# Four changes of order in a one-core kernel: reciprocals behind the key matrices, the gates' series in three parts, the last layer's turns further apart, the last fetch of W_out sooner

## The chip, the cores and the metric
The kernel runs on one core of one Trainium2 chip. The metric is the device time of one execution in microseconds; before, the median of three runs is 3143.19 us (3143.12 to 3145.72). The core has a matmul engine (TensorE, PE), three engines for elementwise work (VectorE or DVE, ScalarE or ACT, GpSimd or POOL), and a fifth, SyncE (SP), which here issues nearly all DMAs. Each of them takes its instructions from a queue of its own, in order, and they wait for each other through semaphores.

## The reference, cut to what matters
Inputs are x (4 x 512 x 512), fside of the same shape, a condition vector per batch, and weights. All is 32-bit floating point. Two layers follow each other:

```python
# layer 1: a bidirectional "wkv" scan, then gated delta-rule attention
ek = exp(min(k, 30)); ekv = ek * v                    # k = v = fside
nf, df = scans of (ekv, ek) forward: a = a*decay + in # nb, db: backward
num = nf + nb - ekv + euk*v;  den = df + db - ek + euk
c = sigmoid(x) * num / max(den, 1e-8) * (0.8 + 0.2*tf)
q, k, v, z = split(c @ W_qkvz.T);  b, a = split(c @ W_ba.T)
q, k, v = silu(causal_conv4(q, k, v))
beta = sigmoid(b);  g = -exp(A_log) * softplus(a + dt_bias)
# 16 query/key heads, 32 value heads, chunks along the sequence:
M = strictly_lower((beta*k) @ k.T * decay);  T = inverse(I + M)
v_c, k_c = T @ (beta*v), T @ (beta*k*exp(g))
for each chunk:                                       # the recurrent part
    v_new = v_c - k_c @ state
    o = (q*exp(g)) @ state + (q @ k.T * decay) @ v_new
    state = state*exp(g_last) + (k*exp(g_last-g)).T @ v_new
x = x + (norm_w * rmsnorm(o) * silu(z)) @ W_out.T
# layer 2: the wkv scan again (r is the new x), then a binarized linear layer
c2 = sigmoid(x) * num2/den2 * (0.8 + 0.2*tf)
x = x + c2 @ (sign(W) * mean|W|).T + bias
```

## The kernel before, in words
The attention is cut into 64 units: one unit is one batch and one query/key head with its two value heads (number n = 16*batch + head). A unit takes the whole sequence of 512 as four chunks of 128. A Python loop runs i from 0 to 65, and each iteration is a list of 22 slots (0 to 21), `plan`, in which steps of different units are interleaved: the key side of unit i+6 (K), convolutions, inverse and queries of unit i (F), the chunk recurrence of unit i-1 (C, four chunks of steps `chunk_r`, `chunk_w`, `chunk_t`), the output norm and its transposes of unit i-2 (O), and the product with W_out of unit i-3 (W). `last_step` ends the work on the last unit and the last batch.

The order in which instructions are issued is written out by hand: the helper class `InOrder` (line 80 is its line, which is why nearly every row of the profile has L80) hands each instruction to its engine and keeps program order. The tile framework places a few instructions otherwise, among them the selects of `gap_mask` on POOL, which it puts where it takes their data to be there.

Steps that matter here:

- `gap_load(n, "d")` (SP) fetches the decay exponents of unit n into tile dkd; `gap_mask` (POOL) masks them, `gap_exp` (ACT) exponentiates. `key_pairs` (PE) makes k·kᵀ in the one PSUM bank of tag "inv", tile ps_kk. `key_root` (POOL) computes the norms' roots and br, nbr, nbe. `key_matrix` (DVE, two halves of four operations) multiplies ps_kk, nbr and dkd into M, and frees the bank. `queries` (PE) then uses that bank for q·kᵀ, tile ps_kq. `key_blocks` (SP) stores M's diagonal blocks, `inverse_load` fetches blocks of the inverse.
- Work of the wkv scan is spread over iterations: heads 3, 4, 5, 7 of a batch carry a 128-column slice of layer 1's scan for the next batch, heads 9, 11, 12, 13 one of layer 2's scan for the same batch; 28 iterations in all. `wkv_under` prepares the denominator, `wkv_over` takes its reciprocal in two halves of 128 x 256 (tile f), `wkv_end` multiplies (into cT for layer 1; for layer 2 it also stores the result, "base", to DRAM).
- The gates of the next batch (beta and g) are computed at head 8, in iterations 8, 24 and 40: `gates_product` (PE, tile ps_ba), `gates_exp`, `gates_series` (DVE: the reciprocal of 1 + exp(-b), and softplus by a series; tiles sp_e, sp_s, sp_p, sp_y), `gates_sum` (PE, ps_g from sp_y), `gates_keep`, `gates_turn` (ps_gt), `gates_rows`. Batch 0's gates are made before the loop.
- `chunk_r` (PE, ps_s) multiplies the state; `chunk_r_end` (DVE) makes r, which `chunk_w` (PE, ps_w) needs.
- Layer 2 is done by `job`s, steps hung onto iterations and slots: `fw_load`, `fw_abs`, `fw_sign` (DVE, fa), `fw_turn` (PE, ps_fw) and `fw_end` prepare the binarized weight in iterations 58 and 59; batches 0 to 2 are finished in iterations 60, 62 and 64 and the one after each: `last_turn` (PE transposes, ps_lx, four per batch), `last_sigmoid` (ACT, sg), `last_mix` (POOL, last_c), `last_product` (PE, ps_f), `last_add` (DVE, then a store on SP). `last_base` and `last_load` fetch their inputs. The last batch is finished in `last_step`.
- `out_start(n, h)` (SP) fetches half h of unit n's rows of W_out (tile wo, two buffers); it stands in slots 13 and 15 for unit O, `out_product` (PE, ps_out) uses it.

PSUM has two banks of tag "pp", three of "pj" (which ps_lx, ps_h, ps_fw, ps_out, ps_g, ps_gt share), one of "inv" and two of "st".

Of the kernel before, what the change touches and what calls it, by code (L numbers as in the profile page):

```python
# [12 lines left out]
ALU = mybir.AluOpType  # L13
# [12 lines left out]
def bc(ap, axis, n):  # L26

    ap = ap.unsqueeze(axis)
    shape = list(ap.shape)
    shape[axis] = n  # L30
    return ap.to_broadcast(shape)
# [9 lines left out]
def kernel(  # L41
# [26 lines left out]
    NC = S // P  # L68
# [14 lines left out]
    V, A, G, T, Q = (InOrder(e) for e in (nc.vector, nc.scalar, nc.gpsimd, nc.tensor, nc.sync))  # L83
    NB = P // BS
    NM = 2 * NC
    NU = B * HQ
# [33 lines left out]
    for i in range(3):  # L120
        t = const.tile([P, NM, P], F32, name=f"inv_t{i}")
        G.memset(t, 0.0)
        inv_t.append(t)
        t = const.tile([P, NM // 2, 3 * BS], F32, name=f"inv_n{i}")
# [21 lines left out]
    with ExitStack() as main:  # L146
# [13 lines left out]
        xs, cT, beta, gsum, eg = {}, {}, {}, {}, {}  # L160
# [40 lines left out]
        nea = const.tile([P, HV], F32, name="nea")  # L201
# [113 lines left out]
        def gates_tile(g, name, tag):  # L315
            t = wkp.tile([P, S], F32, tag=tag, name=f"sp_{name}_{g['b']}")
            return t[:, : NC * HV].rearrange("p (c h) -> p c h", c=NC)
# [13 lines left out]
            V.scalar_tensor_tensor(e, y, -1.0, y, ALU.mult, ALU.min)  # L331
            A.activation(e, e, AF.Exp)

        def gates_series(g):

            b, y, e = g["b"], g["y"], g["e"]
            V.tensor_scalar_add(beta[b], beta[b], 1.0)
            V.reciprocal(beta[b], beta[b])
            s = gates_tile(g, "s", "d")
            V.tensor_scalar_add(s, e, 2.0)  # L340
            V.reciprocal(s, s)
            V.tensor_tensor(s, s, e, ALU.mult)
            V.tensor_tensor(e, s, s, ALU.mult)
            p = gates_tile(g, "p", "ekv")
            V.tensor_scalar_mul(p, e, 1.0 / 19.0)
            for odd in (17, 15, 13, 11, 9, 7, 5, 3):
                V.scalar_tensor_tensor(p, p, 1.0 / odd, e, ALU.add, ALU.mult)
            V.scalar_tensor_tensor(p, p, 1.0, s, ALU.add, ALU.mult)
            V.tensor_scalar_max(y, y, 0.0)
            V.scalar_tensor_tensor(y, p, 2.0, y, ALU.mult, ALU.add)  # L350
            V.tensor_tensor(y, y, bc(nea, 1, NC), ALU.mult)

        def gates_sum(g):
            n = NC * HV
# [680 lines left out]
        def last_add(b, c):  # L1035
# [7 lines left out]
        K, F, C, O, W = AHEAD, 0, -1, -2, -3  # L1043
# [10 lines left out]

            [(slab_turn, K, 1), (out_product, W, 2), (out_product, W, 3), ("wkv", wkv_copy),
             (inverse_1_end, F), (out_scale, O, 0), (gap_exp, F, "t", 0), (chunk_squares, C, 0),
             ("gate", gates_series), ("sub", 2, 22)],

            [(chunk_r, C, 1), (inverse_2, F), (out_add, W, 2),
             (chunk_r_end, C, 1), (out_add, W, 3), (slab_end, K, 1), (chunk_q_end, C, 1),  # L1060
             (gap_exp, F, "t", 1), ("sub", 3, 23)],

            [(project, K, 1, 0), (slab_turn, F, 2), ("wkv", turn_slice, "x"),
             (inverse_2_end, F), (out_scale, O, 1), ("wkv", wkv_bound), ("sub", 4, 24)],

            [(chunk_w, C, 1), (project, K, 1, 1), (head_turn, O, 0), ("gate", gates_sum), (chunk_w_end, C, 1),
             (slab_end, F, 2), ("wkv", wkv_exp), ("wkv", wkv_x),
             (slab_start, F, 3), ("sub", 5, 25)],

            [(project, F, 2, 0), (tap, K, 1, 0), (taps, K, 1), (head_end, O, 0),  # L1070
             ("gate", gates_keep), ("wkv", wkv_mix), ("sub", 6, 26)],

            [(chunk_t, C, 1), (inverse_3, F), ("gate", gates_turn), (chunk_t_end, C, 1), (silu, K, 1),
             ("wkv", wkv_scan, "d", False), (slab_start, F, 0), ("sub", 7, 27)],

            [(project, F, 2, 1), (head_turn, O, 1), (slab_turn, F, 3), ("gate", gates_rows), (inverse_3_end, F), ("wkv", wkv_scan, "d", True),
             (square, K, 1), (chunk_squares, C, 1), ("sub", 8, 28)],

            [(chunk_r, C, 2), (inverse_4, F), (norms, K, 1), (tap, F, 2, 0), (head_end, O, 1), (slab_end, F, 3), (tap, F, 2, 1),
             (chunk_r_end, C, 2), (tap, F, 2, 2), (tap, F, 2, 3), (norms_copy, K, 1), (chunk_q_end, C, 2),  # L1080
             ("wkv", wkv_sum, "d"), (slab_start, C, 4), (slab_start, C, 5), ("sub", 9, 29)],

            [(project, F, 3, 0), (norms_turn, K, 1), (slab_turn, F, 0), (inverse_4_end, F), (silu, F, 2),
             ("wkv", wkv_scan, "n", False), ("sub", 10, 30)],
# [11 lines left out]

            [(chunk_r, C, 3), (key_pairs, K), (tap, F, 0, 0), (slab_end, C, 5), (turn_end, F, 1),
             (tap, F, 0, 1), (chunk_r_end, C, 3), (tap, F, 0, 2), (tap, F, 0, 3),
             (chunk_q_end, C, 3), (inverse_load, F + 1), ("wkv", wkv_over, 0), ("sub", 15, None)],

            [(z_product, C, 0, 0), (turn, F, 3), (key_matrix, K, 0), (silu, F, 0),
             ("wkv", wkv_over, 1), ("sub", 16, None)],

            [(chunk_w, C, 3), (z_product, C, 0, 1), (out_turn, O, 0), (chunk_w_end, C, 3),
             (turn_end, F, 3), (square, F, 0), (key_matrix, K, 1), ("wkv", wkv_end),
             (gap_load, K + 1, "d"), (slab_start, K + 1, 1), ("sub", 17, None)],

            [(z_product, C, 1, 0), (out_turn, O, 1), (out_end, O, 0), (key_blocks, K), ("sub", 18, None)],

            [(chunk_t, C, 3), (norms, F, 0), (queries, F), (z_silu, C, 0), (out_end, O, 1),  # L1110
             ("sub", 19, None)],

            [(z_product, C, 1, 1), (chunk_t_end, C, 3), (norms_copy, F, 0), (queries_end, F, 0), (queries_end, F, 1),
             (chunk_squares, C, 3), (gap_load, F + 1, "t"), ("sub", 20, None)],
# [17 lines left out]
        for pool, tag, count, shape in (  # L1132
# [3 lines left out]
            for i in range(count):  # L1136
                t = pool.tile(shape, F32, tag=tag, name=f"lent_{tag}_{i}")
# [6 lines left out]
        for pool, tag, shape in ((u1p, "nz", [P, NC, 2, HD]), (u1p, "hT", [P, 2, S])):  # L1144
            t = pool.tile(shape, F32, tag=tag, name=f"lent_{tag}")
# [101 lines left out]
        g = {"b": 0}  # L1247
# [44 lines left out]
        first_key(0)  # L1292
        gates_exp(g)
        first_key(1)
        gates_series(g)
        gates_sum(g)
        first_conv(0)
        gates_keep(g)
# [61 lines left out]
        def job(i, slot, f, *args):  # L1360
            jobs.setdefault((i, slot), []).append((f, args))
# [3 lines left out]
        for n in range(KT):  # L1365
            i, slot = at + n // 2, 9 * (n % 2)
            job(i - (slot == 0), (slot - 4) % 22, fw_load, n)
            for more, f in ((0, fw_abs), (1, fw_sign), (3, fw_turn), (4, fw_end)):
                job(i, slot + more, f, n)
        for b in range(B - 1):  # L1370
            i = at + 2 + 2 * b
            for half in range(2):
                job(i - 1, 15 + half, last_base, b, half, b == 0)
            for c in range(NC):
                job(i - 1, 15, last_load, b, c)
                for more, f in ((5, last_turn), (6, last_sigmoid), (8, last_mix)):
                    job(i, more + c, f, b, c)
                late, slot = ((0, 13), (0, 17), (1, 2), (1, 4))[c]
                job(i + late, slot, last_product, b, c)
                job(i + late, slot + 1, last_add, b, c)  # L1380
        for half in range(2):
            job(NU + 1, 6, last_base, B - 1, half, False)

        def last_step():
            n = NU - 1
# [10 lines left out]
        for i in range(NU - W - 1):  # L1396
            b, hq = divmod(i, HQ)
            w, soon = extra(i), extra(i + 1)
            g = {"b": b + 1} if hq == GATES and b + 1 < B else None

            s, half = (i + 2) // GROUP, (i + 2) % GROUP
            s = s if s and half < 2 and s * GROUP < NU else None
            later = []
            for slot, line in enumerate(plan):
                for f, *rest in line:
                    if f == "wkv":
                        if w:
                            rest[0](w, *rest[1:])
                    elif f == "soon":
                        if soon:  # L1410
                            rest[0](soon, *rest[1:])
                    elif f == "gate":
                        if g:
                            rest[0](g)
                    elif f == "load":
                        if s is not None and half == 0:
                            group_load(s)
                    elif f == "sub":
                        if s is not None and rest[half] is not None:
                            group_step(s, rest[half])  # L1420
                    elif f == "store":
                        if s is not None and half == 1:
                            group_end(s)
                    elif 0 <= i + rest[0] < NU:
                        if i == 0 and (f in INVERSE or f == gap_load and rest[0] > K):
                            later.append((f, *rest))
                        elif i or f != inverse_load:
                            f(i + rest[0], *rest[1:])
                for f, args in jobs.get((i, slot), ()):
                    f(*args)  # L1430
                if i == 0 and slot == 13:
                    for n in others:
                        first_matrix(n)
                if i == 0 and slot == 18:
                    for f, *rest in later:
                        f(rest[0], *rest[1:])
# [33 lines left out]
```

## Time and profile before
| | |
|---|---|
| median of 3 runs | 3143.19 us |
| the profiled execution | 3145.25 us, its span 3143.2 us |
| mean granted PE clock | 0.982 of full |
| PE busy | 2991.7 us, 95% |
| DVE / ACT / POOL busy | 66% / 59% / 42% |
| startup (span start to iteration 1) | 196.3 us, of it 75.2 us PE idle |
| an iteration of batch 1 or 2 without extra work | 43.16 us |
| with a slice of layer 1's / layer 2's scan | 45.66 / 45.17 us |
| iterations 8, 24, 40 (gates) | 53.52, 50.79, 50.79 us |
| iterations 58, 59, 60, 62 | 43.24, 47.21, 52.11, 48.05 us |
| iteration 64 and the tail | 87.39 us |

A row of a timeline reads: start and duration in us, engine, line, operation, out<-in by tile names, shapes, how many instructions the row stands for, and in brackets the idle time just before it with what ended it. A row of the waits reads: the waiting engine and tile, what it waited for, then total time, times and the longest in us. DVE's busy time does not say what bounds: an engine that is off PE's path may be idle or late without cost, until PE waits for it.

### The profile page before, as it was taken

What the parts mean: (1) busy time and instruction counts of PE and PEld (TensorE: products, weight loads), DVE (VectorE), ACT (ScalarE), POOL (GpSimd) and SP (SyncE); (2) the same over time, 40 slices, a digit from 0 to 9 for tenths busy, and PEclk for the clock granted to TensorE, in tenths of its full rate; (3) what the DMA queues carried; (4) which work ended last, traced back from release to release, by engine and by line L of the source; (5) the groups of instructions that cost most, each with busy time, mean ns of one, the idle gap of its engine ahead of it and who ended that gap; (6) DMA issues with size and microseconds to landing.
All of it is one profiled execution on the core that took longest, in us unless ns stands there. A gap on an engine that the chain in (4) does not pass through costs nothing.

```text
span 3143.2 us, 57926 instructions
## 1 busy us (share of the span) xinstructions
PE 2991.7 (95%) x20058; PEld 1979.9 (63%) x20058; DVE 2066.1 (66%) x4738; ACT 1861.3 (59%) x5115; POOL 1313.4 (42%) x3044
## 2 busy tenths in 40 slices
PE   6489999999999999999999999999999999999998
PEld 3256666666666666666666666666666666665664
DVE  7546767667665777668766776667765656577642
ACT  2446666666666666556665666566666666655542
POOL 3216354263522646164432646255442515255302
PEclk9689999999999999999999999999999999999999
DMA  3334544444434323332332422332332322333321
GB/s 75 90 87 140 144 122 127 119 141 132 137 111 142 111 68 92 95 94 85 108 104 89 126 69 88 109 91 84 114 94 74 113 83 84 110 89 96 105 84 54
DMA packets 421875, 320.52 MB, mean 102 GB/s; under 512 B 220176, under 2 KB 329232, under 8 KB 421200
## 3 DMA queue, kind: packets, MB, share of 16 engines
q1 hardware_dynamic: 417360, 314.73, 34.5%
q8 instruction: 160, 2.62, 0.4%
q10 hardware_dynamic: 4224, 2.10, 0.3%
q14 instruction: 131, 1.07, 0.1%
HBM read 246.19 MB, written 70.52 MB: 101 GB/s over the span
## 4 chain that ended last, share of the span: by engine, by line
PE 72%; DVE 17%; ACT 8%; issue 2%; DMA 1%; SPq 0%; POOL 0%; ACTq 0%; DVEq 0%; POOLq 0%
PE ps_p L80 20%; PE ps_out L80 13%; PE ps_z L80 11%; DVE y L80 5%; PE ps_w L80 4%; PE ps_s L80 4%; PE ps_o L80 3%; PE ps_kq L80 2%; PE ps_st L80 2%; DVE f L80 2%; PE ps_f L80 2%; PE ps_j L80 2%; PE ps_i L80 1%; PE ps_v L80 1%; ACT y L80 1%
## 5 line engine op out<-in xcount | busy, mean ns | idle before, releaser
L80 PE MATMUL ps_p<-cT,w 128*128 128x512 f32 x2000 | 956.4, 606 | 13.6 <-ACT w L80 13.6
L80 DVE SCALAR_TENSOR_TENSOR y<-ps_p,cw,y 128x511 f32<-128x511 f32 (+2 forms) x768 | 573.2, 746 | 436.3 <-ACT y L80 421.6
L80 PEld LDWEIGHTS ps_p<-cT,w 128*128 128x128 f32 x2000 | 346.7, 191 | 307.7 <-issue 263.4
L80 PE MATMUL ps_z<-w,cT 128*128 128x256 f32 x2048 | 476.5, 379 | 0.0
L80 PE MATMUL ps_out<-wo,hT 128*128 128x512 f32 x1024 | 465.6, 597 | 7.1 <-DMA wo<-wosc 7.1
L80 PEld LDWEIGHTS ps_z<-w,cT 128*128 128x128 f32 x2048 | 373.7, 190 | 42.5
L80 PEld LDWEIGHTS ps_out<-wo,hT 128*128 128x128 f32 x1024 | 185.5, 191 | 194.8 <-issue 189.4
L80 ACT ACT_TABLE_LOAD x137 | 175.8, 1283 | 160.6 <-DVE y L80 115.9
L80 POOL TENSOR_TENSOR L<-L,t 128x30 f32<-128x30 f32 (+14 forms) x450 | 248.7, 553 | 34.9
L80 ACT ACTIVATE qs<-ps_s,eg 128x128 f32<-128x128 f32 x384 | 120.3, 364 | 239.4 <-PE ps_j L80 136.3
L80 POOL TENSOR_TENSOR t<-L 128x30 f32<-128x30 f32 (+14 forms) x450 | 228.3, 507 | 43.8 <-DMA L<-blocks_m 13.9
L80 POOL TENSOR_SCALAR_AFFINE_SELECT dkd<-dkd 128x1024 f32<-128x1024 f32 x64 | 70.0, 1094 | 396.8 <-DMA dkd<-gsc 272.9
L80 ACT ACTIVATE y<-ps_p,cw 128x512 f32<-128x512 f32 x256 | 173.9, 679 | 70.2 <-PE ps_p L80 69.2
L80 POOL TENSOR_TENSOR rs_t_o<-rs_y_o 128x8 f32<-128x8 f32 x192 | 38.7, 202 | 416.9 <-DVE rs_y_o L80 406.9
L80 ACT ACTIVATE junk<-o 128x128 f32<-128x128 f32 x512 | 157.9, 308 | 75.7 <-DVE o L80 67.6
L80 POOL TENSOR_TENSOR rs_t_k<-rs_y_k 128x4 f32<-128x4 f32 x174 | 55.8, 321 | 348.5 <-DVE rs_y_k L80 339.4
L80 ACT ACTIVATE v<-y 128x512 f32<-128x512 f32 x128 | 80.7, 630 | 203.6 <-DVE y L80 201.0
L80 DVE SCALAR_TENSOR_TENSOR o<-o,rs_y_o,nz 128x128 f32<-128x128 f32 x512 | 189.8, 428 | 1.2 <-POOL rs_y_o L80 1.2
L80 DVE TENSOR_TENSOR x<-x,ps_out 128x512 f32<-128x512 f32 x256 | 168.9, 679 | 25.1 <-PE ps_out L80 24.9
L80 DVE SCALAR_TENSOR_TENSOR r<-ps_s,nbe,vb 128x128 f32<-128x128 f32 x384 | 115.8, 343 | 93.1 <-PE ps_s L80 93.1
L80 ACT COPY w<-ps_w 128x256 f32<-128x256 f32 (+1 forms) x346 | 145.4, 431 | 46.6 <-PE ps_w L80 46.4
L80 ACT ACTIVATE dkt<-dkt,gsum 128x128 f32<-128x128 f32 x512 | 162.6, 392 | 17.4 <-POOL dkt L80 17.3
(270 smaller groups left out, 5565.0 us busy)
## 6 DMA issues: line engine op xcount, KB each, us to landing
w<-wsc SPq DMA_DIRECT2D x288, 256.0 KB, 4.9
dkd<-gsc SPq DMA_DIRECT2D x64, 512.0 KB, 4.3
dkt<-gsc SPq DMA_DIRECT2D x64, 512.0 KB, 4.7
wraw<-in_L_attn_W_qkvz_dram SPq DMA_DIRECT2D x96, 256.0 KB, 3.0
wo<-wosc SPq DMA_DIRECT2D x96, 256.0 KB, 3.7
wsc<-w SPq DMA_DIRECT2D x90, 256.0 KB, 2.1
blocks_m<-dkd SPq DMA_DIRECT2D x256, 32.0 KB, 2.5
L<-blocks_m SPq DMA_DIRECT2D x16, 512.0 KB, 4.9
```

The costliest lines, as they stand in the source:

```text
L80: return lambda *args, **kw: tc.keep_in_program_order(op(*args, **kw))
```

## The change
Five edits, all of them of order; nothing is computed differently.

1. `wkv_over` goes from slots 16 and 17 to slots 18 and 19, behind both halves of `key_matrix`, and `wkv_end` from slot 18 to 20. On DVE both reciprocals then stand behind the eight operations of `key_matrix`. On SP the store of base stands behind `key_blocks`, and so no longer ahead of the loads of dkd and of the key weights; with that the framework puts the select of `gap_mask` further ahead on POOL in some iterations.
2. `gates_series` is cut into three parts, in slots 4, 5 and 6 instead of all in slot 3; beta's two operations go to the end of part 2. `gates_sum`, `gates_keep`, `gates_turn` and `gates_rows` move one slot later (`gates_rows` from 9 to 10).
3. `fw_turn` and `fw_end` come 6 and 7 slots after `fw_load`'s base slot instead of 3 and 4.
4. `last_turn`, `last_sigmoid` and `last_mix` of the four chunks stand two slots apart instead of one. ACT loads its function table twice more in each of iterations 60 and 62.
5. The two `out_start` of the last unit, in iteration 65, go from slots 13 and 15 to slot 4.

```diff
-        def gates_series(g):
+        def gates_series(g, part):
             b, y, e = g["b"], g["y"], g["e"]
-            V.tensor_scalar_add(beta[b], beta[b], 1.0)
-            V.reciprocal(beta[b], beta[b])
-            s = gates_tile(g, "s", "d")
+            if part == 0:
+                s = g["s"] = gates_tile(g, "s", "d")
...
+            elif part == 1:
+                p = g["p"] = gates_tile(g, "p", "ekv")
...
+            elif part == 2:
+                p = g["p"]
...
+                V.tensor_scalar_add(beta[b], beta[b], 1.0)
+                V.reciprocal(beta[b], beta[b])
...
-             ("gate", gates_series), ("sub", 2, 22)],
+             ("sub", 2, 22)],
...
-             (gap_exp, F, "t", 1), ("sub", 3, 23)],
+             (gap_exp, F, "t", 1), ("gate", gates_series, 0), ("sub", 3, 23)],
...
-             (inverse_2_end, F), (out_scale, O, 1), ("wkv", wkv_bound), ("sub", 4, 24)],
+             (inverse_2_end, F), (out_scale, O, 1), ("wkv", wkv_bound), ("gate", gates_series, 1),
+             ("sub", 4, 24)],
-            [(chunk_w, C, 1), (project, K, 1, 1), (head_turn, O, 0), ("gate", gates_sum), (chunk_w_end, C, 1),
+            [(chunk_w, C, 1), (project, K, 1, 1), (head_turn, O, 0), (chunk_w_end, C, 1),
              (slab_end, F, 2), ("wkv", wkv_exp), ("wkv", wkv_x),
-             (slab_start, F, 3), ("sub", 5, 25)],
+             (slab_start, F, 3), ("gate", gates_series, 2), ("sub", 5, 25)],
             [(project, F, 2, 0), (tap, K, 1, 0), (taps, K, 1), (head_end, O, 0),
-             ("gate", gates_keep), ("wkv", wkv_mix), ("sub", 6, 26)],
+             ("gate", gates_sum), ("wkv", wkv_mix), ("sub", 6, 26)],
...
-             (chunk_q_end, C, 3), (inverse_load, F + 1), ("wkv", wkv_over, 0), ("sub", 15, None)],
-            [(z_product, C, 0, 0), (turn, F, 3), (key_matrix, K, 0), (silu, F, 0),
-             ("wkv", wkv_over, 1), ("sub", 16, None)],
+             (chunk_q_end, C, 3), (inverse_load, F + 1), ("sub", 15, None)],
+            [(z_product, C, 0, 0), (turn, F, 3), (key_matrix, K, 0), (silu, F, 0), ("sub", 16, None)],
             [(chunk_w, C, 3), (z_product, C, 0, 1), (out_turn, O, 0), (chunk_w_end, C, 3),
-             (turn_end, F, 3), (square, F, 0), (key_matrix, K, 1), ("wkv", wkv_end),
+             (turn_end, F, 3), (square, F, 0), (key_matrix, K, 1), ("wkv", wkv_over, 0),
              (gap_load, K + 1, "d"), (slab_start, K + 1, 1), ("sub", 17, None)],
-            [(z_product, C, 1, 0), (out_turn, O, 1), (out_end, O, 0), (key_blocks, K), ("sub", 18, None)],
+            [(z_product, C, 1, 0), (out_turn, O, 1), (out_end, O, 0), (key_blocks, K), ("wkv", wkv_over, 1), ("sub", 18, None)],
             [(chunk_t, C, 3), (norms, F, 0), (queries, F), (z_silu, C, 0), (out_end, O, 1),
-             ("sub", 19, None)],
+             ("wkv", wkv_end), ("sub", 19, None)],
...
-            for more, f in ((0, fw_abs), (1, fw_sign), (3, fw_turn), (4, fw_end)):
+            for more, f in ((0, fw_abs), (1, fw_sign), (6, fw_turn), (7, fw_end)):
...
-                    job(i, more + c, f, b, c)
+                    job(i, more + 2 * c, f, b, c)
...
+        for h in range(2):
+            job(NU + 1, 4, out_start, NU - 1, h)
...
-                        elif i or f != inverse_load:
+                        elif not (i == 0 and f == inverse_load or i == NU + 1 and f == out_start):
```

More of the change, by code (lines that the diff above doesn't have):

```diff
@@ L332, in gates_exp @@
             A.activation(e, e, AF.Exp)
-        def gates_series(g):
+        def gates_series(g, part):
             b, y, e = g["b"], g["y"], g["e"]
-            V.tensor_scalar_add(beta[b], beta[b], 1.0)
-            V.reciprocal(beta[b], beta[b])
-            s = gates_tile(g, "s", "d")
[L340 to L351, printed above, removed]
+            if part == 0:
+                s = g["s"] = gates_tile(g, "s", "d")
+                V.tensor_scalar_add(s, e, 2.0)
+                V.reciprocal(s, s)
+                V.tensor_tensor(s, s, e, ALU.mult)
+                V.tensor_tensor(e, s, s, ALU.mult)
+            elif part == 1:
+                p = g["p"] = gates_tile(g, "p", "ekv")
+                V.tensor_scalar_mul(p, e, 1.0 / 19.0)
+                for odd in (17, 15, 13, 11, 9, 7, 5, 3):
+                    V.scalar_tensor_tensor(p, p, 1.0 / odd, e, ALU.add, ALU.mult)
+            elif part == 2:
+                p = g["p"]
+                V.scalar_tensor_tensor(p, p, 1.0, g["s"], ALU.add, ALU.mult)
+                V.tensor_scalar_max(y, y, 0.0)
+                V.scalar_tensor_tensor(y, p, 2.0, y, ALU.mult, ALU.add)
+                V.tensor_tensor(y, y, bc(nea, 1, NC), ALU.mult)
+                V.tensor_scalar_add(beta[b], beta[b], 1.0)
+                V.reciprocal(beta[b], beta[b])
         def gates_sum(g):
@@ L1056 @@
              (inverse_1_end, F), (out_scale, O, 0), (gap_exp, F, "t", 0), (chunk_squares, C, 0),
-             ("gate", gates_series), ("sub", 2, 22)],
+             ("sub", 2, 22)],
             [(chunk_r, C, 1), (inverse_2, F), (out_add, W, 2),
              (chunk_r_end, C, 1), (out_add, W, 3), (slab_end, K, 1), (chunk_q_end, C, 1),
-             (gap_exp, F, "t", 1), ("sub", 3, 23)],
+             (gap_exp, F, "t", 1), ("gate", gates_series, 0), ("sub", 3, 23)],
             [(project, K, 1, 0), (slab_turn, F, 2), ("wkv", turn_slice, "x"),
-             (inverse_2_end, F), (out_scale, O, 1), ("wkv", wkv_bound), ("sub", 4, 24)],
-            [(chunk_w, C, 1), (project, K, 1, 1), (head_turn, O, 0), ("gate", gates_sum), (chunk_w_end, C, 1),
+             (inverse_2_end, F), (out_scale, O, 1), ("wkv", wkv_bound), ("gate", gates_series, 1),
+             ("sub", 4, 24)],
+            [(chunk_w, C, 1), (project, K, 1, 1), (head_turn, O, 0), (chunk_w_end, C, 1),
              (slab_end, F, 2), ("wkv", wkv_exp), ("wkv", wkv_x),
-             (slab_start, F, 3), ("sub", 5, 25)],
+             (slab_start, F, 3), ("gate", gates_series, 2), ("sub", 5, 25)],
             [(project, F, 2, 0), (tap, K, 1, 0), (taps, K, 1), (head_end, O, 0),
-             ("gate", gates_keep), ("wkv", wkv_mix), ("sub", 6, 26)],
-            [(chunk_t, C, 1), (inverse_3, F), ("gate", gates_turn), (chunk_t_end, C, 1), (silu, K, 1),
+             ("gate", gates_sum), ("wkv", wkv_mix), ("sub", 6, 26)],
+            [(chunk_t, C, 1), (inverse_3, F), ("gate", gates_keep), (chunk_t_end, C, 1), (silu, K, 1),
              ("wkv", wkv_scan, "d", False), (slab_start, F, 0), ("sub", 7, 27)],
-            [(project, F, 2, 1), (head_turn, O, 1), (slab_turn, F, 3), ("gate", gates_rows), (inverse_3_end, F), ("wkv", wkv_scan, "d", True),
+            [(project, F, 2, 1), (head_turn, O, 1), (slab_turn, F, 3), ("gate", gates_turn), (inverse_3_end, F), ("wkv", wkv_scan, "d", True),
              (square, K, 1), (chunk_squares, C, 1), ("sub", 8, 28)],
@@ L1080 @@
              (chunk_r_end, C, 2), (tap, F, 2, 2), (tap, F, 2, 3), (norms_copy, K, 1), (chunk_q_end, C, 2),
-             ("wkv", wkv_sum, "d"), (slab_start, C, 4), (slab_start, C, 5), ("sub", 9, 29)],
+             ("wkv", wkv_sum, "d"), (slab_start, C, 4), (slab_start, C, 5), ("gate", gates_rows), ("sub", 9, 29)],
             [(project, F, 3, 0), (norms_turn, K, 1), (slab_turn, F, 0), (inverse_4_end, F), (silu, F, 2),
@@ L1294 @@
         first_key(1)
-        gates_series(g)
+        for part in range(3):
+            gates_series(g, part)
         gates_sum(g)
@@ L1413 @@
                         if g:
-                            rest[0](g)
+                            rest[0](g, *rest[1:])
                     elif f == "load":
```

## The prediction
> **What bounds the kernel now.** I read the page's busy times first, then TensorE's (PE's) waits, then timelines around each wait, and last the granted clock in stretches of 3.4 us. The page:
>
> ```profile
> PE 2991.7 (95%) x20058; PEld 1979.9 (63%) x20058; DVE 2066.1 (66%) x4738; ACT 1861.3 (59%) x5115; POOL 1313.4 (42%) x3044
> PEclk9689999999999999999999999999999999999999
> ```
>
> PE is busy for 95% of the span, and its clock is full from the second tenth on. So time is won only where PE stands idle or runs at a lower clock. The waits of PE that the change touches:
>
> ```profile
> PE ps_kq L80 <- DVE dkd L80: 26.4, 17, 1.6
> PE ps_w L80 <- DVE r L80: 9.1, 6, 2.5
> PE ps_out L80 <- DMA wo<-wosc: 7.1, 1, 7.1
> PE ps_lx L80 <- ACT sg L80: 6.2, 3, 3.3
> PE ps_fw L80 <- DVE fa L80: 5.1, 2, 3.4
> ```
>
> Columns: total, times, longest. The reader sees 17 equal stalls of 1.55 us before ps_kq, and a few single ones; together 54 us.
>
> **Part 1: the reciprocals.** The timelines of DVE and PE at the end of iteration 35:
>
> ```profile
> 1791.53 1.74 DVE L80 RECIPROCAL f<-f 128x256 f32<-128x256 f32 x1
> 1793.19 1.03 DVE L80 SCALAR_TENSOR_TENSOR dkd<-ps_kk,nbr,dkd 128x128 f32<-128x128 f32 x4
> 1794.13 1.75 DVE L80 RECIPROCAL f<-f 128x256 f32<-128x256 f32 x1
> 1795.79 1.03 DVE L80 SCALAR_TENSOR_TENSOR dkd<-ps_kk,nbr,dkd 128x128 f32<-128x128 f32 x4
> 1796.87 1.16 PE L80 MATMUL ps_kq<-q,k 128*128 128x128 f32 x8 [1.56 <-DVE dkd L80]
> ```
>
> ps_kq takes the one bank that dkd reads ps_kk from, so it waits for the eighth dkd operation at 1796.8. The changed order on DVE has all eight dkd operations first and both reciprocals behind. ps_kk ended at 1788.4 and nbr at 1788.1, so the eight run from 1791.5 to 1793.6, and PE, free at 1795.31, does not wait. 17 x 1.55 = 26.4 us go. The 11 other iterations with this work have no such stall and gain nothing.
>
> What is late next: DVE's total is the same, so relative to PE it enters the next iteration 1.55 us later. There DVE stands idle for 3.94 us before qe, and POOL's root, which ended at 1496.6 in iteration 28, is needed by the scaling of o at 1499.3: 2.7 us of slack against 1.55. The base store moves behind the stores of the blocks in SP's queue; it waited for the same reciprocals before, so the load of dkd and of w that stood behind it now leave sooner. Ends: 0 (a next wait takes all) to -26.4. I take -26.4, since both slacks are larger than 1.55.
>
> **Part 2: W_out sooner.** The tail:
>
> ```profile
> 3107.30 2.09 SPq L80 DMA_DIRECT2D last_c<-base  x4
> 3109.45 0.97 SPq L80 DMA_DIRECT2D wo<-wosc  x2
> 3106.58 1.07 ACT L80 COPY hT<-ps_h 128x512 f32<-128x512 f32 x2 [13.57 <-PE ps_h L80]
> 3114.06 7.19 PE L80 MATMUL ps_out<-wo,hT 128*128 128x512 f32 x12 [7.08 <-DMA wo<-wosc]
> ```
>
> The two loads of wo move ahead of the last out store and the four last_c loads. They are then held by PE's last reader of the old wo, which ended at 3102.7, so they go out until 3103.7 and land 3.64 us later (3110.42 to 3114.06 in these rows), at 3107.3. hT is there at 3107.65, and ps_out starts at 3107.7 instead of 3114.06: -6.4. What moves behind them, last_c, is issued at 3107.3 as before (the out store ahead of it waits for its sum until 3106.84), lands by 3113.1 at the same 3.64, and is needed at 3115.3 (before: 3123.7, less 8.4): nothing.
>
> The clock there, in stretches (after the times: busy PE, PEld, DVE, ACT, POOL, then granted clock, DMA share, GB/s):
>
> ```profile
> 3107.50:3110.90 3.40, 0.00 (x0) 0.00 (x0) 0.00 (x0) 0.16 (x1) 0.00 (x0) 1.00 0.91 272
> 3110.90:3114.30 3.40, 0.24 (x1) 0.27 (x2) 0.00 (x0) 0.00 (x0) 0.00 (x0) 0.50 0.85 267
> 3114.30:3117.70 3.40, 3.40 (x5) 1.33 (x6) 0.00 (x0) 0.00 (x0) 0.00 (x0) 0.50 0.02 5
> ```
>
> After the idle stretch the clock is half until a busy stretch has passed. The 12 ps_out took 7.19 us, at full clock 12 x 0.43 = 5.2; with 0.7 us of idle instead of 7.1 the clock stays, -2.0. Together -8.4 (-6.4 to -8.4).
>
> **Part 3: the last layer's turns.** Iteration 60:
>
> ```profile
> 2880.76 1.28 ACT L80 ACT_TABLE_LOAD   x1
> 2882.06 0.60 ACT L80 ACTIVATE sg<-ps_lx 128x512 f32<-128x512 f32 x1
> ```
>
> The third turn waited 3.27 us for the first sg, which frees its bank; turns two slots apart put 4 ps_st/ps_o/ps_i groups and 1.7 us of ps_p ahead of the next turn that needs the bank, at about 2882.6, when sg is done. That wait goes, and with it the half clock after it (ps_st and ps_o took 1.06 each, 0.60 elsewhere: about 1.2). So -4.5 in iteration 60, -0.9 in 62 (its wait of 0.94), and -2.2 in 64 (2.04, and some half clock): -7.6. ScalarE gets two table loads more in 60 and two in 62, 4 x 1.28 = 5.1 us, since exp and silu come between sigmoids; ACT is 59% busy and silu's results feed PE several slots later, so I take 0, with 5.1 as the other end.
>
> The Trainium skill ("ScalarE: Activation LUTs", What ACT_TABLE_LOAD costs) speaks against this part: it counts a drain of about 1.38 us beside each load of 1.28. The trace shows none: sg starts 0.02 us after the load. By the page the four loads would cost 10.6 us of ACT, and, if all of it were on the path, the sum below would be 10.6 us less of a gain.
>
> **Part 4: ps_fw.** These turns move three slots back; their waits of 1.77 (iteration 58) and 3.35 (59) go, and the half clock after the second, where four ps_p took 3.62 us instead of 1.88. But fa is late because DVE is late, and behind the moved turn PE meets ps_s, which needs the state from the same DVE queue. I keep -1.1 in 58 and -0.5 in 59: -1.6, ends 0 and -7.6 (5.1, 1.7, and an estimated 0.8 for other matmuls in that half-clock stretch).
>
> **Part 5: the gates.** Iteration 24:
>
> ```profile
> 1277.95 2.58 DVE L80 SCALAR_TENSOR_TENSOR sp_p<-sp_p,sp_e 128x128 f32<-128x128 f32 x8
> 1282.16 0.60 DVE L80 SCALAR_TENSOR_TENSOR r<-ps_s,nbe,vb 128x128 f32<-128x128 f32 x2
> 1282.56 0.75 PE L80 MATMUL ps_w<-r,inv_t 128*128 128x128 f32 x4 [2.50 <-DVE r L80]
> ```
>
> Before, the whole series stands ahead of r. In the changed order r comes about 1.07 us after ps_s starts (as in iterations without gates), so PE goes on at 1280.06 without a wait. It then has ps_w 0.5, ps_p 1.7, ps_h 0.4 and the next ps_p 1.7, and stands before ps_g at about 1284.5. ps_g needs sp_y. DVE after r, from 1278.1: two adds 0.65, part 0 1.83, inverse copies 1.7, o 1.14, part 1 2.87, part 2 1.0: 1287.3. So a wait of 2.8 for sp_y takes the place of 2.50 for r, and PE reaches the next step 0.35 later than before; the taps behind come 2.2 us later (1.13 of it is beta, now behind), into slack of about 2.
>
> In every stretch of 3.41 us in the steady part with 1.97 us or more of PE idle, the clock was half in the next one; with 1.79 or less it was not. The 2.50 here fell across two stretches. A wait of 2.8 has two chances in three of putting 1.97 into one; that costs up to 1.7, so 1.1: +1.5 in each of iterations 24 and 40. In iteration 8 the wait was 1.67, the new one is about 2.5, and ps_gt's later copy holds a bank: +1.9. At startup beta ahead of the taps: +0.3. Together +5.2; ends: -6.7, if all three waits for r go and none comes, and +10, if each new wait also halves the clock and makes the taps late.
>
> The Trainium skill ("TensorE: Matmul & The Clock Gate", Part 1: The HAM clock gate) lets the clock fall only after a whole idle window of about 3.4 us. The trace disagrees: the 3.27 us in iteration 60, with matmuls on both sides, was enough. By the page the gates' new waits would cost no clock, and the sum would be about 3 us better.
>
> **Sum.** -26.4 - 8.4 - 7.6 - 1.6 + 5.2 = -38.8. The profiled execution took 3145.25 us (span 3143.2 and 2.05 around it): 3106.4. It lies 2.06 above the median of the three runs, 3143.19, so against that: **3104 us**.
>
> **Rivals.**
> (a) The gain of part 1 is taken by a next wait. For: DVE is equally loaded and later. Against: the slacks above. Then about 3104 + 26 = 3130.
> (b) The gates gain their waits: 6.7 won instead of 5.2 lost, 3092. For: PE's ps_g could be later than I place it, if more matmuls stand ahead. Against: 4.4 us of PE work and 9.2 of DVE's.
> (c) Slower: the select that masks dkd on POOL. In the changed order of POOL it stands ahead of key_root in six iterations (25, 28, 29 and 41, 44, 45), where before it stood behind; POOL is in order, so if the load of dkd is late, the roots, nbr and with them dkd and ps_kq wait. In before the load left SP at 43 us into these iterations, behind the base store. If it still did, it would land at 47, and key_root (about 5 us from its first operation to nbr) would end at 52 where dkd needs it at 38: ps_kq would come some 11 us late, 6 x 11 = 66 us, 3170. It decides from 6.5 us of delay in each, 38.8 / 6. Against: the base store is no longer ahead; in iteration 26, where none is ahead before either, the load left at 18.4 us and the select ran at 22.6, 5 us before the root, which waits 3.15 us for its input anyway.
> (d) The change does not do what it says: parts 1 and 2 show in the order of the queues, so only a wait that I misread would leave 3137 to 3143.
>
> **How the numbers follow.** A measurement of this kernel tells about 0.2%, 6 us, from no change. My forecast, 3096 to 3115 (it holds the other ends of parts 3 and 4, and 3101 if the gates' new waits fall across two stretches and cost no clock, one chance in three): 0.65. (a), with partial losses, 3115 to 3133: 0.15. (b), 3089 to 3096: 0.08. (c): 0.07. (d): 0.05, of which 0.03 within 0.2%. Faster 0.90, same 0.03, slower 0.07. The range takes the forecast, (a) and half of (b): 3092 to 3131.
>
> **What will show it.** Right: no ps_kq wait for dkd and plain lengths (44.1, 43.6) of those 17 iterations; ps_out about 7 us sooner in the tail at full clock; no ps_lx wait above 1 us in 60; ps_g waiting 2 to 3 us for sp_y in 24 and 40. Wrong: a new wait in the iteration after each of the 17; ps_kq waiting far longer in 25, 28, 29, with POOL's dkd select waiting for its load; PE waiting for v or y in 60 and 62, behind table loads.

## The result, and the profile after

The changed kernel takes 3108.21 us (median of four runs, 3103.34 to 3109.32) against 3144.20 for the kernel before on the same chips: a ratio of 0.9882, 95% interval 0.9865 to 0.9899. It is 36.0 us faster. 3104 was predicted, with 3092 to 3131 as the range.

The page of the profile after (its span is 36.2 us shorter):

```profile
span 3107.0 us, 57961 instructions
PE 2988.3 (96%) x20058; PEld 1978.5 (64%) x20058; DVE 2071.6 (67%) x4738; ACT 1866.0 (60%) x5119; POOL 1314.7 (42%) x3044
PEclk9689999999999999999999999999999999999999
```

PE is nearly as busy as before (2991.7 us); what went is idle time. PE's waits that the change touched, after (total, times, longest):

```profile
PE ps_g L80 <- DVE sp_y L80: 8.2, 3, 2.9
PE ps_s L80 <- DVE state L80: 4.1, 2, 3.8
PE ps_gt L80 <- DVE sp_f L80: 2.7, 1, 2.7
PE ps_w L80 <- DVE r L80: 2.5, 3, 1.2
PE ps_h L80 <- ACT sg L80: 1.0, 1, 1.0
```

The waits of ps_kq for dkd, of ps_out for wo, of ps_lx and of ps_fw are gone from the list. In their place stand ps_g's wait for sp_y, which the prediction gave as the price of the gates, and one of 3.8 us for state, which it named for part 4 without its size.

The end of iteration 35 on DVE and PE, the place shown in the prediction:

```profile
1784.85 2.15 DVE L80 SCALAR_TENSOR_TENSOR dkd<-ps_kk,nbr,dkd 128x128 f32<-128x128 f32 x8
1786.91 3.35 DVE L80 RECIPROCAL f<-f 128x256 f32<-128x256 f32 x2
1788.57 1.16 PE L80 MATMUL ps_kq<-q,k 128*128 128x128 f32 x8
```

The eight dkd operations end at 1787.0, and ps_kq starts at 1788.57 with no wait in brackets.

The tail:

```profile
3074.30 1.18 SPq L80 DMA_DIRECT2D wo<-wosc  x2
3079.04 1.07 ACT L80 COPY hT<-ps_h 128x512 f32<-128x512 f32 x2 [13.57 <-PE ps_h L80]
3079.67 5.42 PE L80 MATMUL ps_out<-wo,hT 128*128 128x512 f32 x12 [0.24 <-ACT hT L80]
```

wo leaves before hT is there, ps_out waits 0.24 us, and the twelve matmuls take 5.42 us instead of 7.19.

Added up over iterations, after less before: startup and iterations 1 and 2 +3.9; the three gate iterations +6.0; the 17 iterations with a stall -27.6; iterations 58 and 59 -1.2; 60 and 62 -5.8; 64 with the tail -11.6. Together -36.2.

### The profile page after: what moved, and what is told of

Its sections match the earlier page's. It is cut to its first block, busy times and chain, and to the rows that moved or that the text cites. A ratio compares the mean times of both kernels' runs of the same rounds, so it can differ in the third digit from the quotient of the medians.

```text
span 3107.0 us, 57961 instructions
## 1 busy us (share of the span) xinstructions
PE 2988.3 (96%) x20058; PEld 1978.5 (64%) x20058; DVE 2071.6 (67%) x4738; ACT 1866.0 (60%) x5119; POOL 1314.7 (42%) x3044
## 4 chain that ended last, share of the span: by engine, by line
PE 88%; DVE 6%; ACT 3%; issue 1%; DMA 1%; SPq 0%; POOL 0%; ACTq 0%; DVEq 0%; POOLq 0%
PE ps_p L80 27%; PE ps_z L80 14%; PE ps_out L80 14%; PE ps_s L80 5%; PE ps_w L80 5%; PE ps_o L80 3%; PE ps_st L80 2%; PE ps_j L80 2%; PE ps_kq L80 2%; PE ps_i L80 2%; PE ps_f L80 2%; PE ps_v L80 2%; PE ps_kk L80 2%; PE ps_h L80 1%; PE psn L80 1%
```

## The experiments

Each is compared with the kernel before or the changed kernel by the lengths of its iterations in the profile and, where several rounds were run, by its time. An iteration's length repeats to 0.1 us, except at startup and where half clock falls in one execution and not in another: iterations 58 and 59 together took 90.45, 88.42 and 90.33 us in three executions that differ only in the tail.

### Part 1 alone, the base store left in its place

```diff
-             (chunk_q_end, C, 3), (inverse_load, F + 1), ("wkv", wkv_over, 0), ("sub", 15, None)],
+             (chunk_q_end, C, 3), (inverse_load, F + 1), ("sub", 15, None)],
...
-             ("wkv", wkv_over, 1), ("sub", 16, None)],
...
-             (turn_end, F, 3), (square, F, 0), (key_matrix, K, 1), ("wkv", wkv_end),
+             (turn_end, F, 3), (square, F, 0), (key_matrix, K, 1), ("wkv", wkv_over, 0), ("wkv", wkv_over, 1), ("wkv", wkv_end),
```

> The kernel before with part 1 alone, and with the base store left where it was in SP's queue (so the loads of dkd and w behind it leave no sooner, and POOL's select stays behind key_root). Theory: DVE's order alone makes the gain; no ps_kq wait for dkd is left, the 17 iterations are 1.62 us shorter each, 27.6 in all, 3116 to 3117 us. Rival: the gain needs the earlier dkd load; then ps_kq or dkd still waits and most of the 27.6 is missing, 3135 to 3144 us.

Measured: 3116.63 us, ratio 0.9909 (0.9895 to 0.9924). Each of the 17 iterations is 1.61 to 1.64 us shorter, 27.6 in all, and no ps_kq wait for dkd is left. So the order on DVE makes the gain by itself; the moves on SP and POOL are not needed for it. Iterations 58 and 59 came out 3.2 us shorter as well (90.45 to 87.25), which was not expected: PE's waits there for r and fa are 1.4 and 0.8 us shorter, and the clock was half for 3.4 us of them instead of 6.8.

### The gates as before, all else changed

The edit undoes the second point of the change.

> The changed kernel with the gates' series in one place as before, all else changed. Theory: the three parts lost 0.4, 3.6 and 2.0 us in iterations 24, 40 and 8, and 0.4 to 3.9 at startup, so this is 6 to 10 us faster than the changed kernel: 3098 to 3102 us. Rival: taking r out from behind the series is a gain and the losses come from elsewhere; then this is up to 6.7 us slower, 3108 to 3115 us.

Measured: 3101.99 us, ratio to before 0.9861 (0.9844 to 0.9877), so 6.2 us faster than the changed kernel. Iterations 8, 24 and 40 return to 53.52, 50.79 and 50.78 us, and the waits for r return:

```profile
PE ps_w L80 <- DVE r L80: 8.6, 5, 2.5
```

Startup with iteration 1 took 242.9 us, as in the changed kernel (242.4), though the startup's gates are here in the order of the kernel before, which took 238.6. Over all runs it took 240.4 to 243.2 us with the changed gates (five executions) and 238.2 to 242.9 with those of before (five). Executions of the same startup differ by more than the 3.9 us, and whether the gates have a part in it is not settled.

### The gates spread over the iteration

```diff
+            if part == 0:
+                V.tensor_scalar_add(beta[b], beta[b], 1.0)
+                V.reciprocal(beta[b], beta[b])
...
+            elif part in (2, 3):
...
+                for odd in ((17, 15, 13, 11), (9, 7, 5, 3))[part - 2]:
...
-        for part in range(3):
+        for part in range(5):
```

Parts 0 to 4 stand in slots 3, 9, 12, 15 and 18, `gates_sum` in 19, `gates_keep` in 20, `gates_turn` and `gates_rows` in 21.

> The changed kernel with the gates' series in five parts over the whole iteration, at places where VectorE stood idle (beta in slot 3, then slots 9, 12, 15, 18), ps_g in slot 19 and what follows it in slots 20 and 21; at startup beta first, as before. Theory: the loss was DVE's queue standing in one lump between r and ps_g; spread out, PE waits neither for r nor for sp_y, iterations 24 and 40 take 43.16 + 4.6 of the gates' own matmuls + 0.25 = 48.0 us and iteration 8 about 51: 14 us less than changed, 3094 us. Rival: 10.6 us more of DVE work in one iteration is late wherever it stands; the waits move to state, r or dkd and iterations 24 and 40 stay at 50 to 51: 3102 us or more.

Measured: 3091.93 us, ratio 0.9830 (0.9815 to 0.9845). Iterations 24 and 40 take 48.03 us, iteration 8 takes 51.50; in none of the three is r or sp_y waited for. Against the changed kernel the three are 13.6 us shorter. The same DVE work costs PE nothing where it stands in gaps, and 2 to 6 us an iteration as a lump, whether the lump is ahead of r or behind it.

### Filling PE's wait for sp_y

```diff
         def gates_sum(g):
...
+            if g["b"]:
+                for k in range(KT):
+                    T.matmul(ps, lhsT=ident, rhs=cT[g["b"]][:, k, :], start=True, stop=True)
             flat = g["y"].rearrange("p c h -> p (c h)")
```

> The changed kernel with four needless matmuls of 128 x 512 (1.7 us) ahead of ps_g in iterations 8, 24 and 40, into ps_g's bank, overwritten by ps_g itself. Theory: PE's wait for sp_y is 1.2 instead of 2.9 us in both, ps_g starts at the same time, the clock is full throughout, iteration 40 falls from 54.4 to 51.2 us and iteration 24 stays at 51.2. Rival: iteration 40 was longer for another reason than the clock; it stays at 54.4, or both get longer by the 1.7 us.

In the changed kernel iterations 24 and 40 have the same wait (2.88 and 2.87 us), yet take 51.21 and 54.40 us. Stretches of the clock around the wait in iteration 40 (busy times, then granted clock):

```profile
1988.10:1991.60 3.50, 1.27 (x9) 1.22 (x10) 3.23 (x11) 0.29 (x1) 0.00 (x0) 1.00 0.00 0
1991.60:1995.00 3.40, 3.40 (x23) 2.43 (x22) 3.33 (x9) 1.52 (x3) 0.00 (x0) 0.50 0.02 5
1995.00:1998.40 3.40, 3.40 (x9) 1.85 (x8) 0.59 (x2) 2.95 (x9) 0.00 (x0) 0.50 0.00 0
```

2.2 us of the wait fell into one stretch, and two stretches at half clock followed. In iteration 24 it was split:

```profile
1281.60:1285.00 3.40, 2.15 (x8) 0.84 (x6) 3.16 (x13) 1.17 (x2) 0.00 (x0) 1.00 0.00 0
1285.00:1288.40 3.40, 1.78 (x14) 1.61 (x14) 3.20 (x9) 0.65 (x2) 0.00 (x0) 1.00 0.00 0
```

The run with the turns one slot apart (below) had the same again: 2.1 us of the wait in one stretch, two at half clock, 54.40 us.

With the filling both iterations take 51.46 us and the clock is full in both. In this run a stretch began at 1988.34, so that without the filling an estimated 2.2 us of iteration 40's wait would have fallen into one stretch, as in the changed kernel. Iteration 40 with the filling:

```profile
1987.52 3.60 PE L80 MATMUL ps_g<-cT,ident 128*128 128x512 f32 x8
1990.95 0.38 PE L80 MATMUL ps_g<-sp_y,tri_le 128*128 128x128 f32 x2
1993.20 1.98 PE L80 MATMUL ps_p<-cT,w 128*128 128x512 f32 x4
```

A matmul of the program is two instructions here, so the filling took 3.4 us and not 1.7; it runs over by 0.25 us, and that is all that iteration 24 shows. ps_p takes 1.98 us, where the changed kernel had 3.78 after the unfilled wait. The extra 3.2 us of iteration 40 are the clock. The run without part 4 (below) shows the other side: the same wait of 2.88 in iteration 40, and 51.22 us with the clock full, since there no more than 1.9 us of it fell into one stretch.

### Part 4 undone

```diff
-            for more, f in ((0, fw_abs), (1, fw_sign), (6, fw_turn), (7, fw_end)):
+            for more, f in ((0, fw_abs), (1, fw_sign), (3, fw_turn), (4, fw_end)):
```

> The changed kernel with part 4 undone: the turns of the last layer's weight 3 and 4 slots after their base slot, as before. Theory: part 4 bought nothing, since iterations 58 and 59 took 87.3 us in the kernel with part 1 alone and 89.3 us in the changed one, where PE waits 3.8 us for the state instead of 3.4 us for fa; so 87 us here too. Rival: part 4 won what was predicted, 1.6 us, and part 1 only hid it; then 58 and 59 together take 90 us or more.

Measured: 89.02 us for the two iterations, against 89.29 in the changed kernel; neither number that was expected. Part 4 won nothing that can be seen: the kernel with it had 6.8 us at half clock there, the one without it 3.4, and a run with it and no half clock (the filled one) took 87.03. What it did is exchange one wait for another. Iteration 59 with part 4:

```profile
2823.83 1.38 DVE L80 TENSOR_SCALAR fa<-fa,al 128x512 f32<-128x512 f32 x1
2827.35 1.21 DVE L80 TENSOR_TENSOR_SCAN ek<-decay,ekv 128x512 f32<-128x512 f32 x1
2831.94 0.60 DVE L80 SCALAR_TENSOR_TENSOR state<-state,eg,ps_st 128x128 f32<-128x128 f32 x2
2832.68 1.19 PE L80 MATMUL ps_s<-state,k 128*128 128x256 f32 x2 [3.78 <-DVE state L80]
```

and without it, where the same DVE lump is met one step sooner:

```profile
PE ps_fw L80 <- DVE fa L80: 5.0, 2, 3.4
```

That the two iterations were at 87.25 with part 1 alone, and 1.8 longer here, is mostly a wait for r in iteration 58 (1.1 us here, none there): the base store's place lets the load of dkt go 2.5 us sooner (0.3 us into iteration 58, and 2.8 with part 1 alone). POOL's select of dkt then runs wholly beside the last two of fa's operations on DVE (1.46 us of overlap instead of 0.65), with the first operation on L behind it, and they take 2.19 instead of 1.42 us. That POOL slows them is argued from their overlap and not tried.

### The last layer's turns one slot apart again

```diff
-                    job(i, more + 2 * c, f, b, c)
+                    job(i, more + c, f, b, c)
```

> The changed kernel with the last layer's turns one slot apart, as before. Theory: the waits for sg come back, iteration 60 takes 52.1 us instead of 47.5, iteration 62 48.0 instead of 46.9, and in iteration 64 a wait of 2.0 us stands in place of 1.0, with half clock after the first and the last: 7 us in all. Rival: the other parts let ACT reach sg sooner; iteration 60 stays below 49 us.

Measured: iterations 60, 62 and 64 are 3.32, 1.11 and 2.94 us longer than in the changed kernel: 7.4 us. The 3.27, 0.94 and 2.04 us of waiting for sg are back, as before the change, whatever the other parts do. Iteration 60 stands at 50.8 and not at 52.1, since this time no half clock followed its wait. The same kernel also prices part 2, which it has and the kernel before hasn't: iteration 64 with the tail is 78.78 us against 87.39, 8.6 less.

### Filling the tail's wait for wo

```diff
             n = NU - 1
+            ps = bank("pj", "ps_fill")
+            for k in range(16):
+                T.matmul(ps, lhsT=ident, rhs=last["w"][:, k % KT, :], start=True, stop=True)
```

> The kernel before with 16 needless matmuls of 128 x 512 (6.9 us) into a bank of their own, where PE waits 7.1 us for wo in the tail. Theory: 6.4 of the tail's 8.4 us are the late loads and 2.0 the clock; here the loads are as late as before, but the clock stays full, and the 12 ps_out take 5.2 us instead of 7.2: 2.0 us less from iteration 64 on. Rival: the 7.2 us were ps_out itself waiting for the second half of wo, and stay.

Again a matmul is two instructions: the filling took 13.8 us instead of 6.9 and ran over the wait, so the end came 3.1 us later and the time says nothing. The twelve ps_out took 5.31 us. The run was made again with 8.

> The kernel before with 8 needless matmuls in the tail instead of 16: each is two instructions on PE, so these fill 6.9 of the 7.1 us in which it waits for wo. Theory: the loads land as before, ps_out starts at the same distance, and runs at full clock: iteration 64 with the tail takes 87.4 less 2.0 = 85.4 us. Rival: the wait and not the clock made ps_out slow; 87.4 us stay.

```profile
3108.67 7.13 PE L80 MATMUL ps_fill<-last_w,ident 128*128 128x512 f32 x16
3115.89 5.39 PE L80 MATMUL ps_out<-wo,hT 128*128 128x512 f32 x12
```

Iteration 64 with the tail takes 85.63 us, 1.76 less than before, though the loads of wo land as late as before. The tail's 8.6 us are 6.8 of lateness and 1.8 of clock.

### The reciprocals twice

```diff
+            V.reciprocal(w["nb"][:, half * S // 2 : (half + 1) * S // 2], den)
             V.reciprocal(den, den)
```

> The changed kernel with each of the two reciprocals made twice (the first time into a tile that is no longer used): 3.4 us more of DVE work behind the key matrices in each of the 28 iterations. Theory: the next iteration has room for it, since DVE stands idle for 2.35 us before qe and for 1.9 before r; at most 1 us per iteration reaches PE, and the ps_kq wait does not come back: up to 28 us slower, near 3115. Rival: the changed kernel stands at the edge, and 2 us or more of each 3.4 come out as PE waits: 56 to 95 us slower.

Measured: one run of 3158.63 us, 50 above the changed kernel's median, between what theory and rival gave. The ps_kq wait did not come back. A new one did:

```profile
PE ps_st L80 <- ACT wd L80: 25.7, 17, 2.2
```

Its place in the iteration after one with a doubled reciprocal (iteration 36; DVE, ACT, PE):

```profile
1821.33 0.42 DVE L80 TENSOR_TENSOR o<-ps_o,qs 128x256 f32<-128x256 f32 x1
...
1821.78 0.31 ACT L80 ACTIVATE junk<-o 128x128 f32<-128x128 f32 x1 [6.45 <-DVE o L80]
1823.00 0.62 ACT L80 ACTIVATE wd<-ps_w,eg 128x128 f32<-128x128 f32 x2
...
1823.67 0.70 PE L80 MATMUL ps_st<-wd,kt 128*128 128x256 f32 x2 [1.87 <-ACT wd L80]
```

The late o holds ACT, which takes its instructions in order, and wd behind it is late for ps_st. Ten of the 17 waits are 1.50 to 1.52 us for 3.36 us of added work, so the changed kernel has about 1.86 us of room there. The rest of the 50 us is mostly half clock: 37.5 us more of it after iteration 2 than in the changed kernel, which is an estimated 19 us of time lost. The gate iterations 24 and 40 lose 8.3 and 5.1 us, iteration 8 loses 1.9.

### A faster version

To the spread gates the preparation of the last layer's weight was added in iterations 52 to 55, whose DVE has room (they carry no scan slice):

```diff
+        early = at - AHEAD
+        job(early, 0, last_tile, "w", [P, KT, D], (bp, "cT"))
         for n in range(KT):
...
+            for when, f in ((10, fw_load), (15, fw_abs), (18, fw_sign), (21, fw_turn), (23, fw_end)):
+                job(early + n + when // 22, when % 22, f, n)
```

> The changed kernel with the spread gates of the run before, and the preparation of the last layer's weight in iterations 52 to 55, one block in each, its DVE operations in slot 18, where DVE stands idle. Theory: the waits and the half clock of iterations 58 and 59 come from fw_sign's four operations ahead of r and state on DVE; away from there the two take 40 and 43 us, 6 us less, and iterations 52 to 55 get only their turns' 0.5 us longer, 2 in all: 3087 to 3089 us. Rival: iteration 59 is late through its scan slice; it stays at 46 or more, and the time is 3092 us.

Measured: 3090.28 us, ratio 0.9826 (0.9809 to 0.9842). Iterations 58 and 59 fell from 89.1 to 81.2 us, more than expected and with no half clock left, but iterations 52 to 56 grew by 5.0: in four of them pss waited 0.59 us for the copy of a turn, 2.4 in all, the turns themselves cost 1.6 in the next version, and 1.0 was not traced. Then `(30, fw_turn), (31, fw_end)`, slots 8 and 9 of the next iteration:

> As the version with spread gates and the weight's preparation in iterations 52 to 55, but the four turns and copies in slots 8 and 9 of the next iteration instead of 21 and 1. Theory: what the version before lost in iterations 53 to 56 was pss waiting for the copy of the turn on ACT (0.59 us each); that goes, iterations 53 to 56 take 43.6 us, 58 and 59 stay at 81 us: 2.5 us faster, 3087 to 3088 us. Rival: the turn finds another wait in its new place and the time stays at 3090 us.

Measured: 3086.15 us, ratio 0.9808 (0.9791 to 0.9824). Iterations 53 to 56 take 43.55 us each. This version is 22 us faster than the changed kernel by the medians, and 23 by the ratios to each one's own runs of before (0.9808 and 0.9882). Its page:

```profile
PE 2983.5 (97%) x20058; PEld 1977.7 (64%) x20058; DVE 2071.0 (67%) x4738; ACT 1870.9 (61%) x5125; POOL 1310.5 (42%) x3044
```

## Why the prediction was right, point by point

| part | predicted | measured | by |
|---|---|---|---|
| 1, reciprocals | -26.4 | -27.6 | part 1 alone |
| 2, W_out sooner | -8.4 | -8.6 | turns one slot apart, against before |
| 3, turns | -7.6 | -7.4 | turns one slot apart, against changed |
| 4, ps_fw | -1.6 | about 0 | part 4 undone |
| 5, gates | +5.2 | +6.0 to 6.2 | gates as before, profile |

The working held in its mechanism for four of five parts.

Part 1: the 17 stalls went whole, 1.62 us each rather than 1.55 (the other 0.07 was not traced). What the prediction named as late next was not the nearest. It looked at qe (3.94 us of idle, now 1.8 to 2.4 behind the 17) and at POOL's root; the doubled reciprocals showed that ACT's squares of o, with wd behind them, come first, with about 1.86 us left. Rival (a) was closer than its two slacks made it look: a further 2 us of DVE work behind the key matrices would have cost.

Rival (c), the select ahead of key_root, was rightly given little. POOL and SP in iteration 25 of the changed kernel:

```profile
1332.79 0.34 SPq L80 DMA_DIRECT2D dkd<-gsc  x1
1338.94 1.10 POOL L80 TENSOR_SCALAR_AFFINE_SELECT dkd<-dkd 128x1024 f32<-128x1024 f32 x1
1342.15 1.04 POOL L80 TENSOR_TENSOR rs_t_k<-rs_y_k 128x4 f32<-128x4 f32 x1 [2.12 <-DVE rs_y_k L80]
```

The load leaves 18.8 us into the iteration, and the root still waits 2.12 us for its own input after the select.

Part 2: the two terms, 6.4 for the loads and 2.0 for the clock, measured 6.8 and 1.8.

Part 3: the mechanism and the sum were right, and the free table loads too: four more of them, and the turns' gain is whole. The terms for iterations 60, 62 and 64 were 4.5, 0.9 and 2.2 and measured 3.3, 1.1 and 2.9; that the total came so near is partly luck, since in that run no half clock followed the wait in 60. Between the profiles before and after, iteration 60 alone is 4.7 us shorter. The Trainium skill's extra drain beside each load ("ScalarE: Activation LUTs", What ACT_TABLE_LOAD costs) doesn't show: in iteration 60 of the changed kernel the function behind a load starts 0.02 us after it.

```profile
2871.60 1.28 ACT L80 ACT_TABLE_LOAD   x1
2872.90 0.60 ACT L80 ACTIVATE sg<-ps_lx 128x512 f32<-128x512 f32 x1
```

Part 4 failed at the step "I keep -1.1 in 58 and -0.5 in 59". The prediction saw that PE would meet ps_s behind the moved turn, but credited a rest all the same. DVE's lump, fw_sign and the scans, sets when PE goes on, whichever of its products PE asks for first. Iterations 58 and 59 became 1.2 us shorter, but they did so without part 4 as well (89.02 against 90.45).

Part 5: the new wait was given as 2.8 us and measured as 2.88, 2.87 and 2.43. That 24 and 40 would get the half clock with two chances in three each came out as one of two; where it came it cost 3.2 us and not 1.7, since two stretches passed at half clock. PE was busy through the whole first one (3.40 us in the row at 1991.60), so "half until a busy stretch has passed" did not hold there. Nor do the bounds behind the two chances in three, 1.97 us of idle and 1.79, hold in all runs. With the gates as before a stretch of iteration 58 with 1.3 us of PE idle was followed by half clock; with the wait filled, two stretches of iteration 59 with 1.95 and 1.82 us were not (busy PE, PEld, DVE, ACT, POOL, then the clock):

```profile
2760.10:2763.50 3.40, 2.07 (x54) 1.57 (x54) 3.40 (x11) 0.81 (x4) 2.85 (x8) 0.99 1.08 339
2763.50:2766.90 3.40, 3.40 (x14) 2.88 (x14) 3.32 (x9) 3.35 (x11) 3.01 (x6) 0.50 0.71 170
...
2824.60:2828.00 3.40, 1.45 (x10) 0.92 (x8) 3.33 (x4) 1.76 (x1) 1.10 (x1) 1.00 0.63 249
2828.00:2831.40 3.40, 1.58 (x7) 1.44 (x8) 2.99 (x6) 2.09 (x8) 2.67 (x3) 1.00 1.03 300
2831.40:2834.80 3.40, 3.15 (x19) 2.62 (x18) 2.49 (x5) 2.42 (x7) 0.00 (x0) 1.00 0.96 276
```

So the two chances in three rest on bounds that other runs do not keep, and what else the clock goes by stays open. The Trainium skill's rule that the clock falls only after a whole idle window ("TensorE: Matmul & The Clock Gate", Part 1: The HAM clock gate) would have made both iterations 51.2 us; iteration 40 of the profile contradicts it, with 2.2 us idle in the stretch before.

The sum was -38.8, against 36.0 less in the medians: the startup (+3.9 in the profile), part 4 and the gates' clock on one side, part 1 and iteration 60 on the other. That these nearly cancel is luck.

## What to carry to other kernels

Where one engine is the bound and another in-order engine feeds it, look for work without a near deadline that stands ahead of work with one: swapping the two here won 27.6 us without taking an instruction away. Work that is moved in one lump only moves the wait to the next product in that queue, as with the gates and the weight; cut it and lay it into that engine's idle gaps, which a timeline of a plain iteration shows. Price a wait on the bound engine with the half clock that may follow it (here behind stretches with 1.3 us of idle and more), and call that part chance.

## What the runs showed of the hardware that was not expected

The same wait, 2.88 us at the same place of the same program, left one iteration at 51.2 us and another at 54.4, where 48.0 is the length without it (the spread gates), by where it fell against the clock's stretches of 3.41 us; where it fell differs between executions. In the steady part the half clock lasted one stretch (3.41 us) or two (6.83), and with the reciprocals twice also three (10.24). No run shows what decides that.

fw_sign's two TENSOR_SCALAR operations on fa took 0.42 and 0.49 us in iteration 52 of the fastest version, where POOL was idle, and 1.44 and 1.38 us in iteration 59 of the changed kernel, where POOL worked on f beside them. The two TENSOR_TENSOR behind them took 1.42 us in both, in iteration 59 beside POOL's short operations on L, and 2.19 beside its select of dkt (iteration 58 without part 4). The Trainium skill ("GPSIMD Engine Reference", 1. Specifications) says that the two engines share their interfaces to the on-chip memory, with contention for some VectorE instructions. The longer durations agree with that, but no run here takes POOL's work away to show it.
